# Layer normalisation ahead of a four-layer graph attention stack: all input rows in one ring of tiles, four row tiles per instruction

## The chip, the cores and the metric

The kernel runs on one NeuronCore of one Trainium2 chip, as a single launch. The metric is the device time in microseconds (us). Beside the plain runs there is one profiled execution, from which every duration below is taken.

The engines are written as in the profile: PE is the matrix engine, with PEld its weight loads; DVE is VectorE, ACT is ScalarE and POOL is GpSimd. SP is SyncE, which in this kernel only issues transfers. Each engine takes its instructions strictly in order; they wait for one another by semaphores.

## The reference

`x` has shape (8, 2048, 64) and `adj` is a 2048 by 2048 matrix of zeros and ones, with few ones and most of them in the first rows and columns. Four layers follow each other, each of the form

```
h = maximum(layernorm(x), 0)          # over the last axis, eps 1e-5
x = x + layer(h, adj)
```

- Layer 0: `scores = h h^T / 8`, masked by `adj`, softmax, times `h`.
- Layer 1: `h W`, with additive scores `a1.h_n + a2.h_m`, a leaky ReLU with slope 0.2, masked softmax, ELU.
- Layer 2: four heads of dot-product attention under `adj` plus the diagonal, with bias rows, a leaky ReLU, a projection, a second attention, and a layer norm with `gamma` and `beta`.
- Layer 3: additive attention again, with a ReLU at the end.

A query whose row of `adj` is empty gets the mean over all rows, since a softmax over equal values is uniform.

## The kernel before

**Layout.** The host passes `x` as 2048 rows of 512 values (8 batches of 64). The rows form 16 tiles of 128 rows; one tile of 128x512 f32 is 256 KB. Because `adj` is sparse, the kernel turns it into lists of neighbours (`lists`, L666 to L762) and gathers neighbour rows from a table in HBM by index. `table[k]` (L128) holds the 2048 normalised rows for one stage, a row N with their mean (for queries with no neighbour), and a zero row N+1 as padding. A tile of queries uses `ROWS[i] + PACKED[i]` gathered 128-row slots, 3 for most tiles and 16 for tile 0. `gather` (L249) issues them from POOL, one indirect DMA each, into `ring`, an SBUF ring of 26 slots (L120). Work on tiles follows the order `MAKING`: 15, 14, 13, 0, 12, 11, 10, 1, ...

**Set-up of layer 0 (L764 to L765).** A first `pipeline` of five stages runs over the 16 tiles. `xin_rows` loads a tile of `x` through SP. `norm_a` (L270) sums each row's 64 values on DVE (L273), scales the sums to means on ACT (L282), subtracts them on POOL (L283) and squares on ACT (L284). `pre_b`, that is `norm_b` (L293), sums the squares on DVE (L296) and makes `1/sqrt(var+eps)` by Ln and Exp on ACT (L297, L299). `pre_c` takes the ReLU on ACT (L337), multiplies by the reciprocal on POOL (L338), and calls `mean_of` (L381): four small matmuls against `ones` (L395) and an addition into `acc` on DVE (L399). `pre_d` stores the tile to `table[0]` (L379). After the last tile `acc` is transposed and the mean row is stored (L402 to L405). Every gather of layer 0 waits for all of `table[0]`, that row included.

**Layer 0 (L766 to L767).** A second `pipeline` of nine stages follows. `load_adj` (L657) loads a tile's rows of `adj` in two halves of 512 KB into the pool tile `a`, which has two buffers, and ACT turns each half into `e` (L664). `lists` finds the neighbours: matmuls build keys (L675, L676), DVE takes maxima (L682 to L694), and further small steps on ACT, PE and DVE produce the indices `idx` and the packing matrices `sel` and `selt`. Tile 0 alone has 16 rounds of maxima (L692, L694). Then come `take0` (gathers), `first0` (scores, L462 to L471), `second` (the weighted sum, L419 on POOL and L424 on PE), `third0`, and the normalisation for layer 1, stored to `table[1]`. With tile `order[WAT]`, the fourth one, `load_adj` also calls `weights_in` (L170): some twenty small loads of weights, of which the `wh` block takes one of the two `a` buffers (L188 to L191) until its matmuls (L194) are done, and three loads of bias rows that POOL issues (L206).

**Order.** The program is written tile by tile, but a scheduler of the framework, which works from its own timeline, sets the order of instructions on each engine, so set-up and lists are interleaved. Hardware-queue transfers use eight semaphores in rotation: SP waits, before each transfer, until the one eight places earlier has landed.

Of the kernel before, what the change touches and what calls it, by code (L numbers as in the profile page):

```python
# [8 lines left out]
F32 = mybir.dt.float32  # L9
# [3 lines left out]
AF = mybir.ActivationFunctionType  # L13
OP = mybir.AluOpType
AX = mybir.AxisListType

P = 128
# [52 lines left out]
def edge_stack(ctx: ExitStack, tc: tile.TileContext, x_in, adj, w1, w1t, a1, wh, wht, bh, wo, bo,  # L70
# [79 lines left out]
    nc.gpsimd.memset(zrow[:, :F], 0.0)  # L150
    nc.gpsimd.memset(zrow[:, F:], NEG)
    nc.sync.dma_start(out=qtab[N:, :].rearrange("r (a c) -> (r a) c", c=QW // 16), in_=zcol)
    for k in range(5):
        nc.gpsimd.dma_start(out=table[k][N + 1:N + 2, :], in_=zrow[:, :table[k].shape[1]])
    for k in (2, 3):
        nc.gpsimd.dma_start(out=table[k][N:N + 1, :], in_=zrow[:, :F])
    for k in (1, 4):
        nc.gpsimd.dma_start(out=table[k][N:N + 1, F:], in_=zrow[:, :B])


# [9 lines left out]
    def weights_in(pool):  # L170

        for t, w in ((wd1, w1), (wd3, w3)):
            nc.gpsimd.memset(t, 0.0)
            nc.sync.dma_start(out=t[:D, :D], in_=w)
            nc.sync.dma_start(out=t[D:, D:], in_=w)
        for u, wt, a in ((u1, w1t, a1), (u3, w3t, a3)):
            w2 = pool.tile([D, 2, D], F32, name="w2", bufs=1)
            nc.sync.dma_start(out=w2[:, 0, :], in_=wt)
            nc.sync.dma_start(out=w2[:, 1, :], in_=wt)
            av = pool.tile([D, 2], F32, name="av", bufs=1)  # L180
            nc.sync.dma_start(out=av, in_=a)
            p = ps_m.tile([P, F], F32, name="m")
            nc.tensor.matmul(p[:, :2], w2.rearrange("j t i -> j (t i)"), av, start=True, stop=True)
            nc.gpsimd.memset(u, 0.0)
            nc.vector.tensor_copy(u[:D, 0:2], p[:D, :2])
            nc.vector.tensor_copy(u[D:, 2:4], p[D:, :2])
        nc.gpsimd.memset(q2, 0.0)
        wh2 = pool.tile([P, N // 2], I32, name="a")[:D, :2 * H * D].bitcast(F32).rearrange(  # L188
            "d (h t c) -> d h t c", h=H, t=2)
        for t in range(2):  # L190
            nc.sync.dma_start(out=wh2[:, :, t, :], in_=wh.rearrange("h d c -> d h c"))  # L191
        p = ps_m.tile([P, F], F32, name="m")
        for h in range(H):
            nc.tensor.matmul(p[:, h * D:(h + 1) * D], wh2[:, h].rearrange("d t c -> d (t c)"), wh2[:, h, 0, :],  # L194
                             start=True, stop=True)
        for t in range(2):
            half = slice(t * D, (t + 1) * D)
            nc.vector.tensor_copy(q2[half, t].rearrange("p h d -> p (h d)"), p[half, :H * D])
        for k in range(2):
            nc.gpsimd.memset(whd[k], 0.0)  # L200
            for t in range(2):
                nc.sync.dma_start(out=whd[k][t * D:(t + 1) * D, t * D:(t + 1) * D], in_=wht[2 * k + t])
            nc.sync.dma_start(out=bhc[:, k:k + 1], in_=bh[k * P:(k + 1) * P].rearrange("(p o) -> p o", o=1))
        nc.sync.dma_start(out=wo_sb, in_=wo.rearrange("(k p) d -> p k d", p=P))
        for t, src in ((bo_b, bo), (gamma_b, gamma), (beta_b, beta)):
            nc.gpsimd.dma_start(out=t, in_=bass.AP(tensor=src.tensor, offset=src.offset, ap=[[0, P], [1, D]]))  # L206

    def heads(t, n=B):
        return t.rearrange("p (b d) -> p b d", b=n)
# [9 lines left out]
    def pipeline(*stages, ahead=(), lag=None):  # L219

        states = {}
        lag = lag or list(range(len(stages)))
        turns = [s for s in ahead] + [s for s in reversed(range(len(stages))) if s not in ahead]
        for n in range(NT + max(lag)):
            for s in turns:
                if 0 <= n - lag[s] < NT:
                    i = order[n - lag[s]]
                    stages[s](i, states.setdefault(i, {}))
# [41 lines left out]
    def norm_a(src, st, centre, eng=nc.vector):  # L270

        s = small.tile([P, B], F32, name="ln_s")
        nc.vector.tensor_reduce(s, heads(src), AX.X, OP.add)  # L273
        st["sq"] = rows_pool[0].tile([P, F], F32, name="ln_sq", bufs=4)
        if centre:
            st["less"] = None
            st["src"] = rows_pool[0].tile([P, F], F32, name="ln_xc", bufs=3)
            if eng is nc.vector:
                eng.scalar_tensor_tensor(heads(st["src"]), wide(s), -INV_D, heads(src), op0=OP.mult, op1=OP.add)
            else:  # L280
                mean = small.tile([P, B], F32, name="ln_m")
                nc.scalar.activation(mean, s, AF.Copy, scale=INV_D)  # L282
                eng.tensor_tensor(heads(st["src"]), heads(src), wide(mean), op=OP.subtract)  # L283
            nc.scalar.activation(st["sq"], st["src"], AF.Square)  # L284
            return
        st["src"] = src
        st["less"] = small.tile([P, B], F32, name="ln_m")
        nc.vector.tensor_scalar(st["less"], s, -INV_D, None, op0=OP.mult)
        for b in range(B):
            nc.scalar.activation(st["sq"][:, b * D:(b + 1) * D], src[:, b * D:(b + 1) * D], AF.Square,  # L290
                                 bias=st["less"][:, b:b + 1])
# [71 lines left out]
    def pre_d(k, u):  # L363

        def f(i, st):
            xh = st["xh"]
            if u is not None:
                p = ps_m.tile([P, F], F32, name="m")
                for j in range(F // P):
                    nc.tensor.matmul(p[:, 4 * j:4 * j + 4], st["xt"][:, j, :], u, start=True, stop=True)  # L370
                pv = p[:, :2 * B].rearrange("p (b t) -> p t b", t=2)
                nc.scalar.copy(f1s[:, i, 0, :], pv[:, 0, :])
                nc.scalar.copy(xh[:, F:], pv[:, 1, :])
            store_rows(k, i, xh)
        return f
# [246 lines left out]
    with tc.tile_pool(name="rows", bufs=2) as rp:  # L622
        rows_pool[0] = rp
        sel_all[0] = rp.tile([P, sum(PACKED) * P], F32, name="sel", bufs=1)
        with tc.tile_pool(name="lists", bufs=2) as pool, \
# [40 lines left out]
            def lists(i, st):  # L666
# [78 lines left out]
                for t0 in range(0, T, step):  # L745
# [7 lines left out]
                    for t in range(n):  # L753
# [7 lines left out]
                nc.scalar.activation(idx[:, at + K:at + K + T], ke, AF.Identity, scale=-1.0, bias=past)  # L761
                nc.scalar.activation(mp, mp, AF.Copy, scale=NEG)  # L762

            pipeline(xin_rows, lambda i, st: norm_a(st["x"], st, True, nc.gpsimd), pre_b,  # L764
                     pre_c(None, nc.gpsimd, 0), pre_d(0, None))  # L765
            pipeline(load_adj, lists, take0, both(first0, xin_rows), second, third0, pre_b, pre_c(u1, None, 1),  # L766
                     pre_d(1, u1), ahead=AHEAD0, lag=LAG0)  # L767

# [1 line left out]
        with tc.tile_pool(name="more", bufs=1) as more_pool[0], \  # L770
                tc.tile_pool(name="ps_w", bufs=1, space=bass.MemoryType.PSUM) as ps_w[0], \
                tc.tile_pool(name="ps_q", bufs=3, space=bass.MemoryType.PSUM) as ps_q:
            order[:] = ORDER1
            nc.sync.dma_start(out=sel_dram[:, :], in_=sel_all[0])
            nc.scalar.mul(bhl, bhc, SLOPE)
            additive(1, wd1, elu_add, pre_b, pre_c(q2), pre_d(2, None), products)
            bounds(0, seen, 0)
# [756 lines left out]
```

## Time and profile before

| what | value |
|---|---|
| median of 3 runs (lowest to highest) | 1488.89 us (1488.5 to 1493.22) |
| the profiled execution's own time | 1486.63 us |
| its span in the trace | 1484.9 us |
| DVE busy | 1143.2 us (77%), 2270 instructions |
| POOL busy | 1042.1 us (70%), 852 instructions |
| ACT busy | 726.6 us (49%), 2466 instructions |
| PE busy | 1205.1 us (81%), 4106 matmuls |
| first gather of layer 0 | 75.3 us |
| first score of layer 0 (L462 on DVE) | 115.3 us |
| first gather of layer 1 | 324.2 us |

The last three rows are starts of instructions, counted from the span's start; they divide the part of the kernel that the change touches. A row of groups reads: line, engine, operation, out<-in with sizes, count; after the bar the busy time and the mean duration in ns; then the idle time just ahead of the group and what ended it. In tables of stretches each engine has its busy time in us and the number of its instructions.

### The profile page before, as it was taken

The numbers are of one execution on the slowest core, as the hardware profiler recorded it, in microseconds if no ns is written. First come the engines' busy times: TensorE is split into PE (matmuls) and PEld (weight loads), VectorE is DVE, ScalarE is ACT, GpSimd is POOL, SyncE is SP. The second block draws the span as 40 slices with busy tenths as digits, with TensorE's granted clock in tenths as the row PEclk, the third lists the DMA queues.
The fourth block names the chain that finished last, engine by engine and source line by source line (L and its number), as shares of the span: only waits on it lengthen the run. The fifth ranks groups of instructions, "written<-read, shape, count | busy, mean of one in ns | idle before, by whom it ended". The sixth has DMA issues, their size and how long they took to land.

```text
span 1484.9 us, 16000 instructions
## 1 busy us (share of the span) xinstructions
PE 1205.1 (81%) x4106; PEld 638.3 (43%) x4106; DVE 1143.2 (77%) x2270; ACT 726.6 (49%) x2466; POOL 1042.1 (70%) x852
## 2 busy tenths in 40 slices
PE   4766888957999843998987999998767888957997
PEld 2633344534554411443432444443333444554654
DVE  6889887824979896999995979862269997955675
ACT  5636686844445732666532545545533446741110
POOL 5647888747764558886879888988287678827640
PEclk9998988967999975999999999999967888956999
DMA  7867665537874487661645454200285353237761
GB/s 213 276 219 251 205 192 173 181 130 226 275 235 178 180 311 274 233 231 50 219 163 168 152 191 169 101 22 8 82 306 155 101 168 128 79 116 232 239 195 53
DMA packets 88621, 262.76 MB, mean 177 GB/s; under 512 B 14828, under 2 KB 16792, under 8 KB 80200
## 3 DMA queue, kind: packets, MB, share of 16 engines
q0 software_dynamic: 35680, 136.59, 29.2%
q1 hardware_dynamic: 52840, 125.06, 24.1%
q8 instruction: 35, 0.57, 0.2%
q14 instruction: 66, 0.54, 0.1%
HBM read 204.41 MB, written 57.18 MB: 176 GB/s over the span
## 4 chain that ended last, share of the span: by engine, by line
PE 34%; DVE 17%; POOL 15%; DMA 13%; ACT 11%; issue 9%; SPq 0%; POOLq 0%; DVEq 0%; ACTq 0%
PE y L857 11%; POOL g L256 8%; PE y L424 8%; DMA g<-table,idx 5%; DMA a<-in_adj_dram 4%; ACT yn L869 3%; POOL wg L419 3%; PE y L848 3%; PE m L914 3%; DVE prod L822 2%; PE m L902 2%; DVE s L826 2%; POOL wh L839 2%; DVE wg L419 1%; DMA x<-xs 1%
## 5 line engine op out<-in xcount | busy, mean ns | idle before, releaser
L256 POOL DMA_INDIRECT g<-table,idx x380 | 365.3, 961 | 218.2 <-issue 103.1
L839 POOL TENSOR_TENSOR wh<-g,w 128x1024 f32<-128x1024 f32 x152 | 288.2, 1918 | 45.9 <-PE y L857 42.7
L424 PE MATMUL y<-wg,ident 128*128 128x512 f32 x336 | 187.2, 681 | 25.7 <-POOL wg L419 20.1
L826 DVE TENSOR_REDUCE s<-prod 128x32 f32<-128x2048 f32 x76 | 172.2, 2285 | 19.9 <-ACT w L828 19.8
L419 POOL TENSOR_TENSOR wg<-g,w 128x1024 f32<-128x1024 f32 (+1 forms) x87 | 147.5, 1705 | 16.2 <-PE y L424 6.7
L857 PE MATMUL y<-wh,ident 128*128 128x512 f32 x272 | 132.9, 612 | 21.9 <-POOL wh L855 19.6
L424 PE MATMUL y<-wg,selt 128*128 128x512 f32 x272 | 146.0, 644 | 1.6 <-POOL wg L419 1.3
L857 PE MATMUL y<-wh,selt 128*128 128x512 f32 x272 | 131.3, 607 | 8.2 <-POOL wh L839 8.2
L869 ACT ACTIVATE yn<-y,rec 128x64 f32<-128x64 f32 x512 | 112.5, 368 | 30.2 <-PE y L857 25.9
L424 PEld LDWEIGHTS y<-wg,ident 128*128 128x128 f32 x336 | 65.2, 212 | 94.0 <-issue 50.6
L438 PEld LDWEIGHTS m<-w,selt 128*128 128x128 f32 x408 | 64.2, 207 | 89.5 <-ACT w L590 24.6
L438 PE MATMUL m<-w,selt 128*128 128x8 f32 (+1 forms) x408 | 62.3, 258 | 49.2 <-ACT w L590 20.6
L419 DVE TENSOR_TENSOR wg<-g,w 128x1024 f32<-128x1024 f32 (+1 forms) x88 | 93.2, 1068 | 10.6 <-PE y L424 6.9
L822 DVE TENSOR_TENSOR prod<-q,g 128x2048 f32<-128x2048 f32 x42 | 95.7, 2278 | 5.8 <-ACT g L820 5.6
L820 ACT COPY g<-g 128x512 f32<-128x512 f32 x76 | 47.7, 628 | 92.7 <-DVE prod L822 84.0
L822 DVE TENSOR_TENSOR prod<-qe,g 128x2048 f32<-128x2048 f32 x34 | 77.4, 2277 | 19.7 <-DMA qe<-qtab,qidx 12.1
L468 PE MATMUL q<-rows,sel 128*128 128x512 f32 x136 | 81.5, 695 | 12.1 <-DVE prod L470 5.6
L857 PEld LDWEIGHTS y<-wh,ident 128*128 128x128 f32 x272 | 51.1, 196 | 87.2 <-issue 54.2
L857 PEld LDWEIGHTS y<-wh,selt 128*128 128x128 f32 x272 | 49.4, 191 | 67.9 <-issue 50.4
L424 PEld LDWEIGHTS y<-wg,selt 128*128 128x128 f32 x272 | 52.5, 207 | 55.8 <-issue 47.6
L902 PE MATMUL m<-att,whd 128*128 128x512 f32 x120 | 63.7, 613 | 14.1 <-ACT att L900 14.0
L482 DVE SCALAR_TENSOR_TENSOR zt<-m,bhc,att 128x512 f32<-128x512 f32 x60 | 44.3, 739 | 38.9 <-ACT att L481 38.9
(247 smaller groups left out, 2671.8 us busy)
## 6 DMA issues: line engine op xcount, KB each, us to landing
qtab<-q SPq DMA_DIRECT2D x16, 1040.0 KB, 4.0
a<-in_adj_dram SPq DMA_DIRECT2D x32, 512.0 KB, 5.6
q<-qtab SPq DMA_DIRECT2D x14, 1040.0 KB, 5.0
table<-xh SPq DMA_DIRECT2D x48, 256.0 KB, 2.4
rows<-table SPq DMA_DIRECT2D x48, 256.0 KB, 4.0
xs<-x SPq DMA_DIRECT2D x48, 256.0 KB, 2.3
x<-xs SPq DMA_DIRECT2D x48, 256.0 KB, 3.1
table<-xh SPq DMA_DIRECT2D x32, 260.0 KB, 2.3
```

The costliest lines, as they stand in the source:

```text
L256: g = nc.gpsimd.indirect_dma_start(out=ring[:, (held[i] + t) % RING, :cols], out_offset=None, in_=table[k][:, :], in_offset=bass.IndirectO ...
L419: eng.tensor_tensor(wg[:, :m].rearrange("p t (b d) -> p t b d", b=B), g[:, :, :F].rearrange("p t (b d) -> p t b d", b=B), w[:, t0:t0 + m, ...
L424: nc.tensor.matmul(y, lhs(i, t), wg[:, t - t0, :], start=(t == 0 and own is None), stop=(t == n - 1))
L438: nc.tensor.matmul(p[:, :cols], selt(i, t), packed[:, t, :], start=(t == 0), stop=(t == T - 1))
L468: nc.tensor.matmul(qe, sel(i, t - K), q, start=True, stop=True)
L820: nc.scalar.copy(g, row(i, t))
L822: nc.vector.tensor_tensor(pr.rearrange("p (b h) d -> p b h d", h=H), q[:, :B * H * D].rearrange("p (b h d) -> p b h d", h=H, d=D), heads(g ...
L826: nc.vector.tensor_reduce(s[:, t - lo, :], pr, AX.X, OP.add)
L839: nc.gpsimd.tensor_tensor(wg, heads(row(i, t))[:, :, None, :].to_broadcast([P, B, 2, D]), w[:, :, 2 * k:2 * k + 2, None].to_broadcast([P, ...
L857: nc.tensor.matmul(st["ys"][j], lhs(i, t), wg[:, 4 * j:4 * j + 4], start=first, stop=(t == n - 1))
L869: nc.scalar.activation(yn[:, b, h, :], st["ys"][j][:, b, h, :], AF.Copy, scale=st["rec"][:, 4 * j + b, 2 * k + h:2 * k + h + 1])
L902: nc.tensor.matmul(p, whd[j // 2], yt, start=True, stop=True)
```

## The change

- The first pipeline is gone. All of `x` is loaded by four transfers of 1 MB, each of four tiles, straight into ring slots 0 to 15, which the gathers use later.
- The normalisation is done in place in the ring, four tiles (a group) at a time. One DVE reduction covers 128x2048 values. Of each group, three tiles are subtracted and multiplied on DVE (with ReLU folded into the multiplication) and one on POOL; the squares go to ring slots 16 to 23.
- The per-row means and reciprocals are written twice, to PSUM for DVE and to SBUF for POOL.
- Each group is stored to `table[0]` by two transfers; the mean row is added up by 16 matmuls per group into one accumulator, and by one DVE addition per group.
- The two pad rows of tables 0, 2 and 3 are written by one transfer each instead of two (tables 2 and 3) or one (table 0, whose row N is overwritten later).
- The three bias rows are loaded by SP, in the program text of layer 1, instead of by POOL in `weights_in`.

Lines before L206 keep their number in the changed kernel; most later ones are two lower in layer 0.

```diff
-    for k in range(5):
-        nc.gpsimd.dma_start(out=table[k][N + 1:N + 2, :], in_=zrow[:, :table[k].shape[1]])
-    for k in (2, 3):
-        nc.gpsimd.dma_start(out=table[k][N:N + 1, :], in_=zrow[:, :F])
+    for k in (0, 2, 3):
+        nc.gpsimd.dma_start(out=table[k][N:N + 2, :].rearrange("(o r) c -> o r c", o=1),
+                            in_=zrow[:, None, :F].to_broadcast([1, 2, F]))
     for k in (1, 4):
+        nc.gpsimd.dma_start(out=table[k][N + 1:N + 2, :], in_=zrow)
         nc.gpsimd.dma_start(out=table[k][N:N + 1, F:], in_=zrow[:, :B])
...
-        for t, src in ((bo_b, bo), (gamma_b, gamma), (beta_b, beta)):
-            nc.gpsimd.dma_start(out=t, in_=bass.AP(tensor=src.tensor, offset=src.offset, ap=[[0, P], [1, D]]))
...
-            pipeline(xin_rows, lambda i, st: norm_a(st["x"], st, True, nc.gpsimd), pre_b,
-                     pre_c(None, nc.gpsimd, 0), pre_d(0, None))
+            C, G, V = F // P, 4, 3
+            groups = []
+            for g in range(NT // G):
+                at = slice(g * G * P, (g + 1) * G * P)
+                xg = ring[:, G * g:G * (g + 1), :F]
+                groups.append(xg)
+                (nc.sync).dma_start(out=xg, in_=x_in[at, :].rearrange("(t p) f -> p t f", p=P))
+            for g, xg in enumerate(groups):
+                at = g * G * P
+                xb = xg.rearrange("p t (b d) -> p t b d", d=D)
+                sq = ring[:, NT + G * (g % 2):NT + G * (g % 2 + 1), :F]
+                bank = ps_y.tile([P, F], F32, name="y")
+                mean_v, r_v = (bank[:, k * G * B:(k + 1) * G * B].rearrange("p (t b) -> p t b", b=B) for k in range(2))
+                stat = pool.tile([P, 4, G, B], F32, name="stat", bufs=NT // G)
+
+                def wide4(t, lo, hi):
+                    return t[:, lo:hi, :, None].to_broadcast([P, hi - lo, B, D])
+
+                nc.vector.tensor_reduce(stat[:, 0], xb, AX.X, OP.add)
+                nc.scalar.activation(stat[:, 1], stat[:, 0], AF.Copy, scale=INV_D)
+                nc.scalar.activation(mean_v, stat[:, 0], AF.Copy, scale=INV_D)
+                nc.vector.tensor_tensor(xb[:, :V], xb[:, :V], wide4(mean_v, 0, V), op=OP.subtract)
+                nc.gpsimd.tensor_tensor(xb[:, V:], xb[:, V:], wide4(stat[:, 1], V, G), op=OP.subtract)
+                nc.scalar.activation(sq[:, :V], xg[:, :V], AF.Square)
+                nc.scalar.activation(sq[:, V:], xg[:, V:], AF.Square)
+                nc.vector.tensor_reduce(stat[:, 2], sq.rearrange("p t (b d) -> p t b d", d=D), AX.X, OP.add)
+                nc.scalar.activation(stat[:, 2], stat[:, 2], AF.Ln, scale=INV_D, bias=eps)
+                nc.scalar.activation(r_v, stat[:, 2], AF.Exp, scale=-0.5)
+                nc.scalar.activation(stat[:, 3], stat[:, 2], AF.Exp, scale=-0.5)
+                nc.vector.scalar_tensor_tensor(xb[:, :V], xb[:, :V], 0.0, wide4(r_v, 0, V), op0=OP.max, op1=OP.mult)
+                nc.scalar.activation(xg[:, V:], xg[:, V:], AF.Relu)
+                nc.gpsimd.tensor_tensor(xb[:, V:], xb[:, V:], wide4(stat[:, 3], V, G), op=OP.mult)
+                for lo, hi in ((0, V), (V, G)):
+                    nc.sync.dma_start(out=table[0][at + lo * P:at + hi * P, :].rearrange("(t p) f -> p t f", p=P),
+                                      in_=xg[:, lo:hi])
+                p = ps_m.tile([P, F], F32, name="m")
+                for c in range(C):
+                    for t in range(G):
+                        nc.tensor.matmul(p[:, c:c + 1], xg[:, t, c * P:(c + 1) * P], ones, start=(t == 0), stop=(t == G - 1))
+                if g == 0:
+                    nc.vector.tensor_copy(acc, p[:, :C])
+                else:
+                    nc.vector.tensor_tensor(acc, p[:, :C], acc, op=OP.add)
...
             order[:] = ORDER1
             nc.sync.dma_start(out=sel_dram[:, :], in_=sel_all[0])
+            for t, src in ((bo_b, bo), (gamma_b, gamma), (beta_b, beta)):
+                nc.sync.dma_start(out=t, in_=bass.AP(tensor=src.tensor, offset=src.offset, ap=[[0, P], [1, D]]))
```

After the last group, `acc` is transposed, copied and stored as the mean row as before.

## Prediction, as it was put on record

> **What bounds the kernel now.** The change ends where layer 0 gets its normalised table, so I cut the trace there: first gather (75.3 us), first score (115.3) and first gather of layer 1 (324.2), and read the busy time between these marks. The columns are PE, PEld, DVE, ACT and POOL, then the granted clock, DMA share and GB/s.
>
> ```profile
> 0.00:30.00 30.00, 10.92 (x24) 2.79 (x24) 18.20 (x57) 17.29 (x37) 13.88 (x43) 1.00 0.67 198
> 30.00:60.00 30.00, 23.71 (x99) 20.39 (x99) 25.70 (x117) 22.47 (x63) 23.84 (x24) 1.00 0.90 300
> 115.30:324.20 208.90, 170.94 (x632) 94.81 (x632) 164.91 (x524) 148.09 (x670) 164.40 (x133) 0.89 0.57 187
> 0.00:115.30 115.30, 70.15 (x254) 46.29 (x254) 88.91 (x398) 62.52 (x161) 60.76 (x89) 1.00 0.74 238
> ```
>
> Up to the first score DVE works 88.9 of 115.3 us; POOL and ACT are half idle. DVE's 26.4 idle us lie mostly early (11.8 in the first 30 us). Next, what POOL waited for at its gathers, from the timeline:
>
> ```profile
> 75.30 1.04 POOL L256 DMA_INDIRECT g<-table,idx  x1 [5.72 <-DMA table<-mr]
> 89.80 0.95 POOL L256 DMA_INDIRECT g<-table,idx  x1 [4.68 <-ACT mbb L762]
> 99.79 0.95 POOL L256 DMA_INDIRECT g<-table,idx  x1 [7.79 <-ACT none L707]
> 115.79 0.95 POOL L256 DMA_INDIRECT g<-table,idx  x1 [6.24 <-ACT selt L739]
> 125.57 2.90 POOL L419 TENSOR_TENSOR wg<-g,w 128x1024 f32<-128x1024 f32 x2
> ```
>
> Only the first gather waits for the table (its mean row). The later ones wait for indices, products of the lists, and POOL's first weighting stands behind them at 125.6. So a table finished sooner brings nothing unless the lists are sooner too. What paces the lists is DVE and the adjacency loads; from the timeline of SP:
>
> ```profile
> 8.96 0.59 SPq L179 DMA_DIRECT2D w<-in_w1t_dram  x1
> 11.89 0.34 SPq L663 DMA_DIRECT2D a<-in_adj_dram  x1
> 22.97 1.32 SPq L191 DMA_DIRECT2D a<-in_wh_dram  x2
> 26.16 0.34 SPq L663 DMA_DIRECT2D a<-in_adj_dram  x1
> 31.58 0.33 SPq L663 DMA_DIRECT2D a<-in_adj_dram  x1
> 37.23 0.33 SPq L663 DMA_DIRECT2D a<-in_adj_dram  x1
> ```
>
> The third half of `adj` leaves at 11.9. After the `wh` load has taken one `a` buffer at 23.0, one half leaves each 5.5 us or so, the next only when the last is consumed. Third, the unit costs:
>
> ```profile
> L296 DVE TENSOR_REDUCE ln_q<-ln_sq 128x8 f32<-128x512 f32 x16 | 10.8, 675 | 5.8 <-ACT ln_sq L284 5.8
> L462 DVE TENSOR_TENSOR prod<-q,g 128x1024 f32<-128x1024 f32 x16 | 19.4, 1218 | 3.3 <-ACT q L459 3.2
> L826 DVE TENSOR_REDUCE s<-prod 128x32 f32<-128x2048 f32 x76 | 172.2, 2285 | 19.9 <-ACT w L828 19.8
> L338 POOL TENSOR_TENSOR xh<-ln_xc,ln_r 128x512 f32<-128x512 f32 x16 | 16.6, 1042 | 21.1 <-ACT ln_r L299 19.6 <-DMA x<-in_x_dram 1.2 <-ACT ln_m L282 0.4
> ```
>
> **DVE.** Removed: 32 reductions of 128x512. One takes 0.675, but four back to back (7.53 us) took 2.46, so 0.61 each: 19.6; with 16 small `acc` steps (1.0 where they overlap) 20.6. Added: 8 reductions of 128x2048 at 2.285 = 18.3; 8 operations of 128x1536. No such size is in the trace; 512 took 0.68 and 1024 took 1.22, a further 0.54, so 1536 is 1.76 and eight are 14.1; with four `acc` steps 0.8 more: 33.2. **Net +12.6 us** (9.4 if the removed ones are taken at their full busy rows, 23.8). The built order of the changed kernel has exactly the same list instructions on DVE ahead of the first score as before, so DVE owes 88.9 + 12.6 = 101.5 us by then.
>
> **POOL.** 32 operations at 1.04 become 8: -25.0 us. The nine pad and three bias issues (about 0.53 each) become seven: -2.7, and a 2.7 us wait for `bo_b` goes. All of it lies where POOL is waiting (12.0 us at 17.9, 5.7 at 69.6), hence worth nothing to the end: what is late next is the index. Here the Trainium skill (GPSIMD Engine Reference, Engine selection) speaks for the change: elementwise work belongs on VectorE, GpSimd being about twice as slow for two inputs. The rows agree in price, 1.04 against 0.59 (1.76 for three), so by the rule 24 tile operations save about 11 us. By the stretch above they cost 14.1, for they go from an engine that waits to the one that is awaited. I take the latter.
>
> **ACT.** 16 times 1.91 (L282, L284, L297, L299, L337: 0.19, 0.61, 0.29, 0.19, 0.63) = 30.6 becomes four times 3.8 (a square of 128x1536 about 1.5, by 0.61 at 512 and 1.06 at 1024) = 15.3. ACT is not the bound: 0, except for its place in the queue, below.
>
> **Loads.** The same 4.2 MB. The skill (DMA: Bandwidth & Descriptors, Bandwidth) says to batch to 1 MiB or more; its fit of 2.0 us plus bytes over 436 GB/s makes 16 transfers of 256 KB 42 us and four of 1 MB 18, a gain of 24 us if they ran singly. Here six of 256 KB in flight already moved 313 to 381 GB/s (stretches of one us, 3 to 6), so I count no gain. There is a loss: the first DVE sum waits for 1 MB (about 6.5 us instead of 3.6), and all 4.2 MB stand ahead of `adj`. At 313 GB/s from 2.0 us the groups land at about 6.5, 10, 13 and 16, the first two halves at 17.6 and 19.3 (before: ACT took them at 10.8 and 12.3).
>
> **SP, the queue passed.** In the changed order all 14 weight loads, six `x` tiles and the three bias rows stand ahead of the third half. So the bias rows are not in layer 1; they cost three issues of about 0.58 here. Each issue waits for the transfer eight places back, so the weight loads stall on the groups and the first halves until 19.3. Then 15 issues of 0.45 to 0.6 follow, and with landings of 4.5 us for small loads (the `whd` rows) the third half leaves at about 29 instead of 11.9. ACT's small bias step (L775), which waits for `bhc`, sits ahead of Ln of group 0: idle to about 27. The squares of groups 2 and 3 stand behind the fifth half (lands about 40): done about 44. Last multiplication on DVE about 50, group 3's matmuls (16 at 0.22) to 56, mean row landed about 61: **first gather about 62**, 13 us sooner.
>
> **Sum.** By 59 us DVE has done 3.6 (constants) + 33.2 + 7.7 (lists of tiles 15 and 14) = 44.5, idle 14.5. It has 57.0 left. Before, it had 45 us of work left at 60 us and idled 10.3 of the 55.3 to the score, 4.5 of it for the third layer's weights. I take 6 (3 to 10). First score: 59 + 57 + 6 = 122, against 115.3: **+6.7**. The weightings wait for the same list steps, and in the 209 us that follow nothing is removed, with PE, DVE and POOL all at 79 to 82%; so the delay passes to the first gather of layer 1, about 331. Later layers keep their work; the scheduler changes some of their order, which I count as 0 with 4 us either way. Profiled time 1486.6 + 7 = 1493.6; the median stands 2.3 above it: **1496**.
>
> **The rivals.**
> - *Slower, by DVE's added work* (0.50): 1496, own range 1490 to 1503.
> - *Slower, by the loads* (0.12): the third half leaves 17 us later, and with `wh` holding a buffer the seventh to eleventh halves go singly at 5.5 us each. By my walk the sixteenth is in at about 95, ahead of its need at 103. If that cover of 8 us is gone, by 1.5 us more on each of ten single steps, the score moves 7 more: 1503. For it: `adj` heads the chain of waits up to 116 us.
> - *No change* (0.17): the set-up fills holes. If ACT isn't held for `bhc` and the fifth half, DVE idles 8 instead of 14.5 in the set-up: 101.5 + 8 + 6 = 115.5, 1489. Or POOL (79%) sets layer 0's middle and absorbs it.
> - *Faster, by unbroken lists* (0.21): the set-up comes as a block, and then no DVE step waits for ACT or POOL tile by tile. It decides where total idle to the score falls below 26.4 - 12.6 = 13.8 us. With 6 left, the score is at 107.5: -7.8, so 1481. Against: 4 us of start are certain, and tile 0's packing holds 2.7 of ACT waits.
>
> **How the numbers follow.** A measurement here tells 0.3%, 4.5 us, from no change: slower 0.62, same 0.17, faster 0.21. The range 1479 to 1508 takes in both middle values of the rivals with their order noise.
>
> **What would show it.** Right: third half at about 29, first gather at about 62 but first score at 118 or later, first gather of layer 1 later by as much; DVE's total up 9 to 13 us, POOL's down about 28. Wrong: a first score before 111 (then DVE's idle was the thing), an unchanged 324 with a late score (absorption), or a difference that arises after 330 (order in later layers).

## The result and the profile after

The changed kernel takes 1507.34 us (median of 8 runs, 1500.69 to 1512.29), the kernel before 1488.7 us beside it (8 runs): **ratio 1.013 [1.0103, 1.0156]**, 18.6 us slower. The forecast was +7.3. The direction was right, the size was not. The profiled execution of the changed kernel took 1503.27 us, with a span of 1501.5, so +16.6 in the span. Ratios here and below are of undisturbed executions alone, and of the one trace that caught a slow one (run e16 below) only the set-up is read.

| mark (us from the span's start) | before | after | forecast |
|---|---|---|---|
| third half of `adj` leaves | 11.89 | 25.87 | about 29 |
| first gather of layer 0 | 75.30 | 69.25 | about 62 |
| first score | 115.33 | 131.36 | 122 |
| DVE busy / idle up to it | 88.9 / 26.4 | 100.0 / 31.3 | 101.5 / 20.5 |
| first gather of layer 1 | 324.24 | 341.65 | about 331 |
| DVE busy in all | 1143.2 | 1160.8 | +9 to +13 |

First the table of stretches, in the order of columns used for the kernel before (PE, PEld, DVE, ACT and POOL busy, granted clock, DMA share, GB/s):

```profile
0.00:30.00 30.00, 7.06 (x24) 4.26 (x24) 26.11 (x24) 16.54 (x32) 14.54 (x40) 1.00 0.72 243
30.00:60.00 30.00, 23.86 (x108) 22.43 (x109) 13.79 (x25) 9.04 (x20) 2.08 (x2) 1.00 0.74 255
0.00:131.36 131.36, 72.04 (x254) 46.57 (x255) 100.03 (x371) 50.53 (x113) 33.60 (x60) 1.00 0.63 207
131.36:341.65 210.29, 173.54 (x632) 96.73 (x632) 168.12 (x523) 147.91 (x670) 164.39 (x135) 0.87 0.58 187
```

The first 30 us are better for DVE than before (idle 3.9, was 11.8). Then it turns round: from 30 to 60 us DVE works 13.8 us where it worked 25.7, while PE is as busy as before (23.9 of 30, was 23.7). The whole loss stands at the first score (+16.0). The middle of layer 0 adds 1.4 us to it, and the rest of the program takes 0.8 off. So a delay passed on one to one here, as the prediction had it.

What POOL waited for at its gathers, from the timeline:

```profile
69.25 1.04 POOL L254 DMA_INDIRECT g<-table,idx  x1 [20.82 <-PE k L674]
99.06 0.94 POOL L254 DMA_INDIRECT g<-table,idx  x1 [16.28 <-ACT idx L702]
121.83 0.94 POOL L254 DMA_INDIRECT g<-table,idx  x1 [21.83 <-ACT none L705]
141.56 2.91 POOL L417 TENSOR_TENSOR wg<-g,w 128x1024 f32<-128x1024 f32 x2
```

The table is no longer what the first gather waits for: it waits for PE's key matmul (L674), a step of the lists. Why a key matmul comes so late is in PE's own timeline:

```profile
48.31 13.78 PE L800 MATMUL m<-ones,g 128*128 128x1 f32 x64 [6.14 <-issue]
61.96 0.59 PE L673 MATMUL k<-e,lift 128*128 128x512 bf16 x1
```

Two groups' mean matmuls stand in one block of 13.78 us, and the key matmuls stand behind it in PE's order. The block began as DVE's multiplication of the third group ended (46.46 + 1.75 = 48.21). Ahead of it PE stood idle for 6.1 us, although the `e` of the next half was ready at 43.91. DVE and ACT at that time:

```profile
46.46 1.75 DVE L791 SCALAR_TENSOR_TENSOR g<-g,y 128x1536 f32<-128x1536 f32 x1
55.31 0.16 DVE L804 TENSOR_TENSOR acc<-m,acc 128x4 f32<-128x4 f32 x1 [3.69 <-PE m L800]
62.13 0.16 DVE L804 TENSOR_TENSOR acc<-m,acc 128x4 f32<-128x4 f32 x1 [6.67 <-PE m L800]
63.01 0.70 DVE L680 MAX8 c<-k 128x8 f32<-128x512 f32 x1 [0.71 <-PE k L674]
```

```profile
33.43 1.06 ACT L662 ACTIVATE e<-a 128x1024 bf16<-128x1024 int32 x1 [7.39 <-DMA a<-in_adj_dram]
42.87 1.04 ACT L662 ACTIVATE e<-a 128x1024 bf16<-128x1024 int32 x1
63.44 1.06 ACT L662 ACTIVATE e<-a 128x1024 bf16<-128x1024 int32 x1 [15.67 <-PE k L673]
```

DVE waits 10.4 us for the two small sums behind the block. ACT cannot convert the next half of `adj` for 15.7 us, since PE has not read the last one, and so SP cannot load one either (two halves at 34.5 and 35.7 are left out here):

```profile
25.87 1.77 SPq L661 DMA_DIRECT2D a<-in_adj_dram  x2
43.93 0.34 SPq L661 DMA_DIRECT2D a<-in_adj_dram  x1
64.52 0.33 SPq L661 DMA_DIRECT2D a<-in_adj_dram  x1
```

The mean's PE work itself did not grow. Its group is 27.6 us in the changed kernel and 28.7 before, 128 records each. It was spread over sixteen tiles, with waits for POOL between them, and DVE never waited for its sums; now it comes in two blocks of 13.78 us (from 26.67 and from 48.31).

### The profile page after: what moved, and what is told of

Its sections match the earlier page's. It is cut to its first block, busy times and chain, and to the rows that moved or that the text cites. A ratio compares the mean times of both kernels' runs of the same rounds, so it can differ in the third digit from the quotient of the medians.

```text
span 1501.5 us, 15833 instructions
## 1 busy us (share of the span) xinstructions
PE 1204.1 (80%) x4106; PEld 637.1 (42%) x4106; DVE 1160.8 (77%) x2242; ACT 714.7 (48%) x2418; POOL 1012.4 (67%) x823
## 3 DMA queue, kind: packets, MB, share of 16 engines
q1 hardware_dynamic: 52952, 125.16, 23.7%
## 5 line engine op out<-in xcount | busy, mean ns | idle before, releaser
L422 PE MATMUL y<-wg,ident 128*128 128x512 f32 x336 | 186.8, 677 | 19.5 <-POOL wg L417 13.8
L915 ACT ACTIVATE yn<-y,rec 128x64 f32<-128x64 f32 x512 | 112.0, 368 | 28.7 <-PE y L903 16.4
L436 PEld LDWEIGHTS m<-w,selt 128*128 128x128 f32 x408 | 64.9, 207 | 99.5 <-issue 25.9
L422 PEld LDWEIGHTS y<-wg,ident 128*128 128x128 f32 x336 | 65.1, 211 | 88.2 <-issue 53.4
L903 PEld LDWEIGHTS y<-wh,ident 128*128 128x128 f32 x272 | 51.1, 198 | 88.4 <-issue 53.1
L894 PE MATMUL y<-rows,ident 128*128 128x512 f32 x104 | 58.7, 652 | 16.1 <-DMA rows<-table 13.4
```

The costliest lines, as they stand in the source:

```text
L422: nc.tensor.matmul(y, lhs(i, t), wg[:, t - t0, :], start=(t == 0 and own is None), stop=(t == n - 1))
L436: nc.tensor.matmul(p[:, :cols], selt(i, t), packed[:, t, :], start=(t == 0), stop=(t == T - 1))
L894: nc.tensor.matmul(st["ys"][j], ident, xb[:, 4 * j:4 * j + 4], start=True, stop=False)
L903: nc.tensor.matmul(st["ys"][j], lhs(i, t), wg[:, 4 * j:4 * j + 4], start=first, stop=(t == n - 1))
L915: nc.scalar.activation(yn[:, b, h, :], st["ys"][j][:, b, h, :], AF.Copy, scale=st["rec"][:, 4 * j + b, 2 * k + h:2 * k + h + 1])
```

## The experiments

Two theories came first. *Work*: DVE's 11 us more set-up work is the delay. *Block*: PE's block of mean matmuls is. A third, *loads*, blames the late halves of `adj`. Later runs call block and late halves together the *gates*. Times are compared as ratios only, for the kernel before took 1530 to 1535 us beside the first fifteen runs and 1488.49 beside the last three. Marks are of one execution each; for the same kernel the first score differed by 3 us (115.33 and 112.14 before, 131.36 and 134.37 after).

| run | third half | first gather | first score | DVE busy / idle to it | gather of layer 1 | ratio [95%] |
|---|---|---|---|---|---|---|
| before, again (e8) | 10.56 | 72.98 | 112.14 | 89.5 / 22.7 | 324.17 | 0.9971 [0.995, 0.9992] |
| after, again (e5) | 25.80 | 68.89 | 134.37 | 100.3 / 34.1 | 342.30 | 1.0119 [1.0098, 1.014] |
| e1 mean of one group | 26.50 | 57.20 | 124.16 | 100.4 / 23.8 | 327.20 | 0.9993 [0.997, 1.0017] |
| e2 one tile of four on DVE | 25.84 | 65.90 | 131.92 | 92.8 / 39.2 | 351.93 | 1.0117 [1.0061, 1.0173] |
| e3 before, 12 tiles on DVE | 11.16 | 78.23 | 129.11 | 105.2 / 23.9 | 335.33 | 1.0045 [1.0027, 1.0062] |
| e4 pads and bias alone | 12.12 | 70.41 | 114.05 | 91.9 / 22.2 | 328.12 | 1.0041 [1.0019, 1.0063] |
| e6 mean by rows | 26.23 | 62.84 | 129.45 | 101.0 / 28.4 | 341.18 | 1.0103 [1.0086, 1.012] |
| e7 after, `wh` apart | 26.37 | 68.83 | 134.52 | 101.1 / 33.4 | 346.48 | 1.0073 [1.0046, 1.01] |
| e9 sums on POOL | 26.04 | 67.78 | 128.90 | 101.2 / 27.7 | 345.00 | 1.0125 [1.009, 1.016] |
| e10 the same, no tiles on DVE | 25.64 | 82.82 | 120.64 | 88.4 / 32.2 | 335.35 | 1.0038 [1.0022, 1.0055] |
| e11 before, `wh` apart | 10.82 | 74.04 | 110.64 | 89.6 / 21.1 | 321.65 | 0.9998 [0.9978, 1.0017] |
| e12 x in 16 loads | 21.91 | 66.00 | 131.29 | 100.2 / 31.1 | 340.93 | 1.0125 [1.009, 1.0159] |
| e13 sums on POOL, early `adj` | 20.47 | 66.71 | 118.45 | 101.0 / 17.5 | 340.44 | 1.0076 [1.0055, 1.0097] |
| e14 the same, no tiles on DVE | 19.78 | 80.61 | 124.12 | 91.3 / 32.9 | 331.25 | 1.0087 [1.0055, 1.012] |
| e15 before, early `adj` | 12.40 | 85.60 | 130.31 | 91.7 / 38.6 | 343.73 | 1.0059 [1.0038, 1.008] |
| e16 no DVE tile work | 27.18 | 54.24 | 118.15 | 88.2 / 29.9 | | 1.006 [1.0041, 1.008] |
| e17 the same, no gates | 23.92 | 65.16 | 109.07 | 89.2 / 19.9 | 323.28 | 0.9973 [0.9954, 0.9992] |
| e18 mean of one group, early `adj` | 20.36 | 60.84 | 113.72 | 100.6 / 13.1 | 337.27 | 1.0073 [1.0047, 1.01] |

The kernel before against itself came out at 0.9971, so a difference under some 0.4% is not read.

**The two kernels again (e5, e8)**, unchanged, as a base for the marks:

> The changed kernel itself, on the same chip as the experiments beside it. All theories: 1.013 of the time before (interval 1.009 to 1.017), the mean matmuls of the last two groups in one block of about 14 us, first gather about 69, first score about 131. The block theory (PE's block of mean matmuls holds the key matmuls that stand behind it) takes it as the base for the run with rows of sums.

> The kernel before itself, for the marks of this chip. All theories: 1.000 within 0.003, first gather about 75, first score about 115, first gather of layer 1 about 324 to 328. If its stretch from first score to layer 1's gather is near 214 here, the stretch of the run with the pad and bias edits alone (214.1) is this chip's own; if it is near 209, that run's order is to blame for 5 us.

The first score is 22.2 us later here: 10.9 of it DVE's work and 11.4 its idle time. In the first pair it was 11.1 and 4.9. So the work is steady and the idle part is not.

**e1: the mean of one group.** Under `if g == 0`, the rest left out:

```
-                for c in range(C): ... matmul(p[:, c:c + 1], ...)   # every group
+                if g == 0: ... the same 16 matmuls and the copy
```

> Leaves out the mean matmuls and additions of groups 1 to 3, so the mean row holds group 0 alone (48 of 64 matmuls, 20.7 of 27.6 us on PE). Three theories of the 16.1 us by which the first score is late (131.4 against 115.3). Block theory: the last 64 matmul records stand as one block of 13.8 us on PE from 48.3, with tile 14's keys behind them, and DVE idles 10.4 us for it. Then the first score comes at about 122 and the kernel gains 8 to 10 us, to about 1.006 of before. Work theory: DVE's 11.3 us of additional set-up are what counts, and they stay; gain at most 2 us. Load theory: the third half of adj leaves at 25.9 instead of 11.9 and the later ones follow; that stays too, gain at most 3 us.

The time is that of the kernel before, which is more than the block theory asked for. DVE's idle time up to the first score is 10 us less than in e5, its work the same. The middle of layer 0 was also the shortest of all runs, 203.0 us. The block matters; but how much of this gain is the block's, e18 puts in doubt below.

**e2: one tile of four on DVE.** `C, G, V = F // P, 4, 1`; the other three go to POOL.

> V = 1: of four tiles one is centred and scaled on DVE and three on POOL. DVE sheds 8 times (1.70 - 0.61) = 8.7 us; POOL's eight operations grow from 1.04 to about 3.1 us. Work theory: first score 8.7 earlier, at about 123, kernel at about 1.007 of before. Block theory: nothing gained, since the block of mean matmuls stays; the groups may even finish 2 to 4 us later through POOL, so 1.013 to 1.015. Load theory: no change, 1.013.

7.5 us of DVE work were gone and the first score came only 2.5 us sooner: 5.1 us more idle took their place, half of it behind the block (12.8 us of waits there, 10.3 in e5). Work on DVE alone does not explain the delay while the block stands there.

**e3: the kernel before with the work, without the block.**

```
-  norm_a(..., nc.gpsimd), pre_b, pre_c(None, nc.gpsimd, 0)
+  norm_a(..., nc.gpsimd if i % 4 == 3 else nc.vector), pre_b, pre_c with the same choice
```

> The kernel before with its tile-by-tile set-up, but 12 of the 16 tiles centred and scaled on DVE: 24 operations of 128x512 move there at 0.61 each, 14.6 us more DVE work; loads, mean matmuls and their spreading stay. Work theory: the first score moves from 115.3 to 127 to 130 and the kernel to about 1.009. Block theory and load theory: neither cause is there; within 3 us, 1.000 to 1.002.

The first score came 17 us later than in e8, nearly all of it busy time (15.8), yet the kernel lost 0.45%, some 7 us. Work alone costs, but not the whole.

**e4: pads and bias rows alone.** The first, second and last hunks of the diff, in the kernel before.

> The kernel before with only the pad rows and the bias rows of the change. All three theories: no effect, first score within 2 us of 115.3, 1.000. If the three bias issues on SP delay the adjacency halves enough to matter, the load theory would have 2 to 4 us here.

All theories had 0 here. The ratio is at the edge of what is read, and the gather of layer 1 comes 4 us later than in e8 with DVE's idle time up to the first score unchanged; so some 4 to 6 us of the loss may belong to this part, though half of the 4 us lies in the middle of layer 0, where the kernel before varies as much by itself (208.9 and 212.0 us; 214.1 here). No later run follows that up.

**e6: the mean by rows.**

```
-  matmul(p[:, c:c + 1], xg[:, t, c * P:(c + 1) * P], ones, ...)   # 16 per group
+  matmul(p[0:1, :], ones, xg[:, t, :], ...)                       # 4 per group, then ACT copy, POOL add
```

> The changed kernel, with the mean row formed by four matmuls of 512 columns per group against one column of ones (16 in all, where there were 64 small ones of two passes each), copied by ACT and added by POOL; nothing is left out. Block theory: the last two groups' matmuls take PE about 7 us instead of 13.8, the first score comes 5 to 8 us sooner (124 to 126), and the kernel is at 1.002 to 1.008 of the time before. Work theory (DVE's 11.3 us of added work set the score): the first score stays within 2 us of 131, time 1.011 to 1.014. Load theory (late adjacency halves): likewise within 2 us, for the loads keep their place.

The first gather was 6 us and the first score 4.9 us sooner; the time moved by 0.16%, within the intervals. The block theory asked for 5 to 8 us of the score and 1.002 to 1.008: the score all but came, the time did not.

**e7 and e11: `wh` apart**, in the changed kernel and in the one before:

```
-  wh2 = pool.tile([P, N // 2], I32, name="a")[:D, :2 * H * D].bitcast(F32)...
+  wh2 = w_all.rearrange("p n b -> p (n b)")[:D, :2 * H * D]...
```

> The changed kernel, with the wh block loaded into the weights' own tile, so that both adjacency buffers stay with the adjacency. Load theory: the halves after the sixth go two at a time, and the first score comes 5 us or more sooner, time about 1.008. Block theory and work theory: first score within 2 us of 131, time 1.011 to 1.015.

> The kernel before, with the wh block loaded into the weights' own tile, so that both adjacency buffers stay with the adjacency. Load theory (the halves that go singly set the lists): first score 3 us or more sooner than 112 to 115, time 0.993 to 0.998. Two-term account: DVE sets the lists, first score within 2 us, time 0.998 to 1.003.

The first score stayed in both (134.5; 110.6), so a missing `adj` buffer is not what delays it. e7's time is better by 0.46% with no mark before layer 1 to show for it: expected of no theory, and left open.

**e9: sums on POOL.**

```
+  nc.gpsimd.tensor_tensor(s2, xg[:, 0:2], xg[:, 2:4], op=OP.add)
+  nc.gpsimd.tensor_tensor(s2[:, 0], s2[:, 0], s2[:, 1], op=OP.add)
-  for t in range(G): matmul(p[:, c:c + 1], xg[:, t, ...], ones, start=(t == 0), stop=(t == G - 1))
+  matmul(p[:, c:c + 1], s2[:, 0, ...], ones, start=True, stop=True)
```

> The changed kernel, with each group's four tiles added together on POOL (one addition of 128x1024 and one of 128x512, about 3.1 us in a time when POOL waits) ahead of the mean's matmuls, of which there are then 4 per group (16 in all, 32 records) in place of 16 (64, 128 records); nothing is left out. Two-term account (half of the delay is DVE's 11 us of added work, half is idle of DVE behind PE's block of 13.8 us): PE's work for the mean falls from 27.6 to 7 us, first gather about 62, DVE's idle to the first score falls from 31 to 34 to 22 to 26, first score 122 to 126, time 1.003 to 1.008 of before. Work alone: first score 129 to 134, time 1.010 to 1.014. Block alone: first score 115 to 118, time within 0.003.

The mean's group on PE, by lines of the first 80 us:

```profile
L802 PE MATMUL m<-ones,g 128*128 128x1 f32 x32 | 7.1, 344 | 4.8 <-POOL g L799 4.8
```

The block is gone: DVE's idle time from 40 to 60 us fell from 9.8 to 2.9 us. But 6.6 us of idle still stood between 60 and 80, the first score gained 5.5 us only, and the time nothing. So the block was not the only gate.

**e10: no tiles on DVE.** e9 with both DVE operations, and the ACT steps that feed them, dropped and POOL's widened to `xb[:, 0:G]`; nothing is left out.

> As the run with sums on POOL, and all four tiles of a group are centred and scaled on POOL (128x2048, about 4.1 us each, eight in all), none on DVE; nothing is left out. Two-term account: DVE's work to the first score is 100.2 - 14.1 = 86, with an idle of 24 to 28 (POOL's chain per group is longer), first score 110 to 114, time 0.995 to 1.003. Work alone: likewise, 0.997 to 1.003. Block alone: the same first score as in the run with sums on POOL, within 2 us. If POOL becomes the bound (33 + 12 us of set-up on it), the first gather is after 75 and the first score after 118.

DVE's work is that of the kernel before; its idle time is 9.5 us more than in e8. Each group now passes through two POOL operations of 128x2048 (3.6 us each), which may be why; that was not tested. Of the forms that leave nothing out this is the fastest, and still no faster than the kernel before.

**e12: x in sixteen loads** of 256 KB, the ring slots unchanged:

> The changed kernel, with x loaded by sixteen transfers of 256 KB into the same ring slots. Load theory by size (a transfer of 1 MB is what pays): the last group lands later, and the kernel is at 1.014 to 1.02 of before. Load theory by place: the twelve more issues on SP (about 0.5 us each) put the third adjacency half at 30 or later. The two-term account: no difference of more than 2 us in the first score, time 1.010 to 1.014.

No difference in time, as forecast: neither the size nor the number of the loads matters here. Against the load theory by place, the third half left 4 us sooner, not later; it brought no time while the block stood there.

**e13 to e15: both gates away.** e9 and `wh` apart, with the fourth tile's weight loads issued by POOL (`nc.gpsimd.dma_start` in `weights_in` for all but `w3t` and `a3`); then with no tiles on DVE as in e10; then the load edits alone in the kernel before.

> The changed kernel with sums on POOL ahead of 16 mean matmuls, the weight loads of the fourth tile issued by POOL instead of SP, and wh in the weights' own tile: neither the block on PE nor the late adjacency halves are left, and nothing is left out. Gate account (what idles DVE is the block and, once it is gone, the third half at 26 us behind the weight loads): the third half leaves at 18 to 20, DVE's idle to the first score falls from 28 to 20 to 24, first score 120 to 124 (100 of work), time 1.003 to 1.008. Rival, idle is in the small steps of the lists themselves: first score stays at 127 to 130, time 1.009 to 1.013.

> As the run before it, and all centring and scaling on POOL. Gate account: DVE's work to the score 86, idle 22 to 28, first score 108 to 114, at or before that of the kernel before (112 to 115), time 0.995 to 1.002. Rival (POOL's chain of 4.1 us operations paces the set-up): first score 118 to 121 as with POOL sums and no DVE tiles alone, time 1.003 to 1.006.

> The kernel before with the weight loads of the fourth tile issued by POOL and wh in the weights' own tile. Gate account: the kernel before had its third half at 11.9 us already, so DVE's idle changes by less than 3 us, time 0.996 to 1.003. Rival (loads hold the lists in the kernel before as well): first score 5 us or more sooner, time below 0.996.

e13 is the clearest run for the gates: with the third half at 20.5 us, DVE idles 17.5 us up to the first score, and that score comes at 118.5, 15.9 us sooner than in e5. But less than half of it reaches the time (0.43%, 6.6 us, at the edge of what is read). Against e9, which lacks the block too, DVE's idle time fell by 10.2 us, so the late halves count beside the block:

```profile
0.00:118.45 118.45, 52.54 (x160) 26.27 (x160) 101.00 (x375) 51.32 (x114) 57.34 (x85) 0.99 0.70 233
```

e14 and e15 missed what was expected of them: with the weight loads on POOL's queue besides its tile operations, the first gather came at 80.6 and 85.6, and the score later with it.

**e16 and e17: DVE's eight operations of 128x1536 left out**, so twelve of sixteen tiles are neither centred nor scaled; first in the changed kernel, then in that of e13.

```
-  nc.vector.tensor_tensor(xb[:, :V], xb[:, :V], wide4(mean_v, 0, V), op=OP.subtract)
-  nc.vector.scalar_tensor_tensor(xb[:, :V], xb[:, :V], 0.0, wide4(r_v, 0, V), op0=OP.max, op1=OP.mult)
```

> The changed kernel with DVE's eight operations of 128x1536 left out, so twelve of the sixteen tiles are neither centred nor scaled; the block on PE and the order of the loads stay. Sum (work and idle add up): first score 134 - 14 = 120, time 1.002 to 1.006. Cover (the work lies in the wait for the block): first score 129 or later, time 1.009 or more.

> As the run before it, but from the kernel with sums on POOL, early adjacency halves and wh apart: neither DVE's added work nor the two gates are there (twelve tiles are neither centred nor scaled). Sum: first score 118 - 14 = 104 (86 of work, 18 of idle), 8 us before that of the kernel before; if the time follows the first score, it is 0.994 to 0.997 of before; if PE at its granted clock sets the middle of layer 0, the gain is given back there and the time is 0.998 to 1.004.

With e5 and e13 these are the four corners:

| ratio to before | with the gates | without |
|---|---|---|
| with DVE's work | 1.0119 (e5) | 1.0076 (e13) |
| without | 1.006 (e16) | 0.9973 (e17) |

The work costs 0.6 to 1.0% (9 to 16 us), the gates 0.4 to 0.9% (7 to 13 us), each the less while the other is there. Together they are 1.46%, 22 us, a little more than the loss itself; neither alone makes it up. By the intervals each of these differences is good to about 0.3%. The upper two runs stand beside a kernel before of 1530 us and the lower two beside one of 1488; the changed kernel is at 1.0119 and 1.013 beside the two, but e13 was run beside the first alone.

**e18: the mean of one group, with early `adj`.** e1 and the load edits of e13.

> The changed kernel with the mean matmuls of groups 1 to 3 left out (the mean row holds group 0's sum alone), the weight loads issued by POOL and wh apart; DVE's work stays. Gate account: first score 115 to 119, as in the run with POOL sums and early adjacency (118.5), and time at or below 1.002, for the run with one group's mean and late adjacency stood at 0.9993. Rival (that run owed its time to the order its scheduler chose): time 1.004 to 1.010, with a first score below 120 all the same.

The rival's case: a first score at 113.7, 10 us sooner than in e1, and a time 0.8% worse. The stretches of the two, up to the first score and from there to layer 1; e1:

```profile
0.00:124.16 124.16, 52.95 (x158) 26.14 (x159) 100.41 (x368) 51.53 (x113) 33.82 (x60) 0.99 0.67 222
124.16:327.20 203.04, 171.11 (x633) 94.86 (x632) 164.41 (x523) 148.38 (x670) 164.13 (x133) 0.89 0.59 192
```

e18:

```profile
0.00:113.72 113.72, 51.93 (x163) 26.55 (x163) 100.61 (x372) 51.99 (x115) 42.17 (x76) 1.00 0.72 239
113.72:337.27 223.55, 182.53 (x630) 97.43 (x629) 165.26 (x520) 147.72 (x669) 164.48 (x134) 0.82 0.54 176
```

DVE, ACT and POOL did the same work within a us in the middle; PE had the same matmuls, but they took 11 us longer, at a granted clock of 0.82 instead of 0.89, and the stretch is 20.5 us longer. What was gained before the first score was given back there.

## Why the prediction was right in sign and too small

- **What bounds it, right.** The lists, not the table, pace layer 0: the first gather came 6 us sooner and the first score 16 us later.
- **DVE, right up to the first score.** Owed 101.5 us, measured 100.0; added 11.1, forecast 12.6. The total grew by 17.6, outside the 9 to 13 that were named; the other 6.5 arose later, 4 of them in one step (below). The estimated size, 1.76 us for 128x1536, measured 1.75, and the reduction of 128x2048 2.28:

```profile
L787 DVE TENSOR_REDUCE stat<-g 128x32 f32<-128x2048 f32 x4 | 9.0, 2278 | 3.4 <-ACT g L785 3.4
L791 DVE SCALAR_TENSOR_TENSOR g<-g,y 128x1536 f32<-128x1536 f32 x4 | 6.9, 1744 | 0.0
L783 DVE TENSOR_TENSOR g<-g,y 128x1536 f32<-128x1536 f32 x4 | 6.8, 1748 | 5.2 <-ACT y L782 5.2
```

- **POOL and the rule on elementwise work, right.** POOL lost 29.7 us of work, and the kernel got slower all the same. e16 and e17 price the 14 us that DVE took over at 9 to 16 us of time; e3, with 15.8 us more DVE work in the kernel before, at 7. Giving it back to POOL in groups of four (e10) takes off 0.87% against e9, but DVE's idle time is then larger than in the kernel before.
- **Loads, right.** e12 with sixteen loads differs by less than the intervals. The gain of 24 us was an estimate from a fit that the skill's page gives for transfers issued by GpSimd; these are SP's, and nothing was counted for it.
- **SP, right in mechanism.** Third half at 25.9, forecast 29; bias rows ahead of it. The issues at 14.66, 15.94 and 17.43 waited for the last group and the first two halves, each eight places back.
- **The failed step: the idle term of the sum, 14.5 + 6 = 20.5 us, and in it "group 3's matmuls (16 at 0.22) to 56".** The forecast took 5.9 us of DVE's idle time off; the measured idle time grew by 4.9, to 31.3 (20.1 by 60 us, 11.2 after it). 10.4 of the 31.3 are the two waits behind PE's block, and for these the sum had nothing. A matmul against `ones` in f32 is two records here; the 64 records of two groups took 13.78 us, so 0.43 us for each of 32 matmuls. The step counted one group at half its price, 3.5 us ("to 56" left it 6), and did not ask what stands behind these matmuls in PE's order. Group 3's end came at about 62, and until then no key matmul ran. The prediction has sums for DVE, POOL, ACT, the loads and SP, and none for the order on PE; a block has to be read in order, not by its share (PE was busy for 70 of 115 us).
- **How much of that is the block's.** Without the two waits the idle time is 20.9 us, the forecast's 20.5, but in part by luck: 11.9 by 60 us for 14.5, and 9.1 after it for 6. And the runs give the block less than the trace does: with the block gone and the late halves still there (e9) idle was 27.7, and only with both gone (e13) 17.5. So the late halves, behind the weight loads on SP, cost more than the sum had for them, too. In time, taking the block alone away brought nothing that can be read where nothing was left out (e6, e9; e1's 1.3% is in doubt by e18); with the halves early as well it brought 0.4 to 0.9%.
- **"The delay passes to the first gather of layer 1", right for this pair** (+16.0 to +17.4) but not as a rule. Taking idle away before the first score moved the first gather of layer 1 by little (e13 against e5: 15.9 sooner became 1.9; e18 against the changed kernel's trace: 17.6 became 4.4). DVE's busy time up to that gather, plus 69 to 74 us of idle, gives its place in before, after, e5, e8, e13, e17 and e18: 254 + 70 = 324 and 268 + 73 = 341 for the two kernels; it isn't a law, for over all runs that idle time is 62 (e1) to 88 us (e2). On that count, found after the fact, the sum should have credited no gain of idle: 12.6 would have stood alone.
- **Later layers at 0, right**: -0.8 us.
- The rival by DVE's work was the right one in kind, and its own range ended at 1503. The one by the loads had a part too, not through `wh` (e7, e11): in the changed kernel the block kept the halves back from 44 to 64 us, and without the block the late halves still cost DVE 10 us of idle time (e9 against e13). "Faster" needed DVE's idle time to fall below 13.8 us, and it was 31.3; "no change" had holes to fill, or a middle of layer 0 that absorbs the delay, and the middle grew by 1.4 us.

What stays open: why e1 is as fast as the kernel before while e18, with an earlier first score, is not; the two were run beside kernels before of 1535 and 1488 us, and e1 was not repeated beside the second. Each edit also changes the order that the scheduler gives to later instructions, and no run here held that order fixed. No variant beat the kernel before: e17 leaves work out, and e11 equals it.

## What to carry to other kernels

When a step's work is gathered into bigger pieces, add up what each piece now holds in every in-order queue, and look for what stands behind it; for a spread of 29 us of small matmuls DVE never waited, for two blocks of 13.8 us it waited 10.4 us. Put a price on a matmul by its records in the trace, not by one instruction. Idle time that a change removes ahead of a long stretch with three engines at 80% may come back in that stretch; of work added on DVE more stayed (in e3 11 of 17 us at the first gather of layer 1).

## What the runs showed of the hardware

**DVE stood still behind POOL.** One small step of DVE took 4.03 us in the changed kernel, 4.00 in e5, 5.11 in e2 and 4.38 in e12, 2.13 in e15, 0.69 in e13, and 0.18 to 0.20 in the kernel before and the other runs. DVE and then POOL in the changed kernel, and DVE in the kernel before:

```profile
268.15 4.03 DVE L1058 TENSOR_SCALAR ok<-over 128x48 f32<-128x48 f32 x1
```

```profile
267.36 1.06 POOL L281 TENSOR_TENSOR ln_xc<-x,ln_m 128x512 f32<-128x512 f32 x1
268.36 3.76 POOL L417 TENSOR_TENSOR wg<-g,w 128x1024 f32<-128x1024 f32 x2
```

```profile
258.95 0.18 DVE L1012 TENSOR_SCALAR ok<-over 128x48 f32<-128x48 f32 x1
```

It begins while POOL works and ends at 272.18, when POOL's third operation in a row ends (272.12). The Trainium skill (SBUF — State Buffer, section "SBUF: two separate sides") says that POOL and some of DVE's operations share a pair of ports by an exclusive lock, held for a whole instruction. The rows agree: in all six long cases the step ends 0.04 to 0.06 us after an operation of POOL. They show more: the wait lasted over three POOL instructions. It need not: in e17 the step began at 260.95, beside POOL too, and was through in 0.20 us where one operation of POOL gave way to the next (261.09 and 261.03). This is 4 of the 17.6 us that DVE's busy time grew by; what it cost in time no run here tells.

**Small matmuls do not speed PE up.** In e6 PE's key matmuls came 0.22 us apart after the block of 128x512 ones, and about 0.4 us apart in the changed kernel (61.96, 62.34, 62.76) after 13.8 us of unbroken 128x1 ones. PE in e6:

```profile
26.80 8.06 PE L799 MATMUL m<-g,ones 128*1 128x512 f32 x16 [0.41 <-issue]
34.80 0.39 PE L673 MATMUL k<-e,lift 128*128 128x512 bf16 x1
35.03 0.38 PE L674 MATMUL k<-keys,every 65*128 65x512 bf16 x1
```

The skill (TensorE: Matmul & The Clock Gate, section "What's actually happening") has PE at half rate until it has been busy for about 3.4 us. The trace agrees for wide matmuls; for 128x1 ones, four times that long was not enough. The granted-clock column doesn't tell this: it stood at 1.00 in the changed kernel's slow set-up and at 0.72 in e6's quicker one.

**The granted clock and the middle of layer 0.** Its length times the mean granted clock is 179 to 186 us in all nineteen traces that are read there (203.04 at 0.89 in e1; 223.55 at 0.82 in e18), while the length alone ranges over 20 us. That fits a stretch which PE paces at the clock that it is given; whether a lower clock makes the stretch longer, or one order of work brings both, is not shown. What sets the clock these runs do not show either: the kernel before had 0.89 in one execution and 0.87 in another.
